# A graph layer with segment maxima: which engine makes the one-hot blocks of a slot's first and last chunk, when a search product is issued, and how a list's words are packed

## The chip, the cores and the metric

The kernel runs on one core of a Trainium2 chip. The metric is the device time of one execution in microseconds (us). TensorE is called PE in the profile, VectorE DVE, ScalarE ACT, GpSimd POOL and SyncE SP.

## The reference

```python
theta_x = (x[dst] - x[src]) @ theta_w.T + theta_b
phi_x = x[src] @ phi_w.T + phi_b
e = relu(theta_x + phi_x)
out = segment_max(e, dst, num_segments=6250)      # empty segments: 0
y = layernorm(x + out)
```

x has 6250 nodes of 256 features; there are 100,000 edges, sorted by dst. The part of an edge that depends on its source is a row of B = x @ (phi_w - theta_w).T, so what has to be done for each node is the maximum over its edges of gathered rows of B; the node's own product with theta_w and the biases are added after it.

## The kernel before, in words

The nodes come in two parts. The first 618 nodes (**part 1**) have their edges gathered row by row: POOL issues an indirect DMA for each step (`gather`, L527 to L538), and VectorE keeps a running maximum, one operation a step (`run_steps`, L690). The other 5632 nodes, 128 partitions x 44 (**part 2**), take two ways together:

- **Slots.** The source rows are cut into 17 slots of 383 rows. For each node at most one edge of each slot is chosen (`choice`, L1025, two slots at a time, all on VectorE). TensorE then fetches the chosen rows by products with one-hot matrices (`slot_halves`, L1095). A slot is worked in six chunks of nodes, five of 1024 and a last one of 512: 17 x 6 = 102 **parts** in a fixed order. For a chunk the chosen row numbers are loaded (`want`, L1108), a one-hot tensor `hot` of three blocks of 128 rows is made, and for each of two halves of the features 3 blocks x 2 terms x 2 widths = 12 matmuls go into a PSUM tile `ps_f` (6 for a chunk of 512); VectorE takes the maximum of it into `acc` (L1139; for the first slot ScalarE copies, L1137). The last slot has one block, not three. `hot` has two buffers, `ps_f` three.
- **The list.** Edges that no slot took are left over. VectorE packs them to a list: marks and a running count (L1232 to L1240), words with a distance (L1244 to L1257), eleven moves that close the gaps (L1261 to L1276), the owner's number (L1280). The words go to DRAM (L1283), POOL fetches each partition's 256 of them (L1291), and then issues 256 gathers of rows of B (`gather_2`, L1335), each followed by a short `pause` (an IOTA, L537). VectorE runs maxima over them (L699), two groups of eight behind the gathers. In the middle stage the program ties list and slots together: between two list steps it issues as many halves of chunks as the share of the list that is done asks for (`halves_until`), and VectorE's maxima and list steps are held in that order by hand.

When the list has ended its last rows are stored, POOL gathers the results of part 2 (44 gathers of `maxima`), and the shares of nodes are summed, normalised and stored. The last slot's six parts stand at the end of the slots, and VectorE takes their maxima after the list's last step.

**Who makes a hot block.** The number in `dve_hots[0]` says how many of the three blocks VectorE makes, with one comparison (L1114). ScalarE makes the rest in two operations: |row - number| for each block (L1116), then max(0, 1 - that) over all its blocks at once (L1119). The number is 0 for the first 19 parts (slots 0 to 2 and the first chunk of slot 3), 1 from there on, and is set to 0 again (L1582) when four groups of the list are left, which is ahead of the last seven parts before the last slot: slot 14's last chunk and all of slot 15. The trace has 70 such operations on VectorE.

**The search of places.** `node_place` (L855) finds where in part 1 the last edge of a node lies, in five calls: VectorE makes a hot (L858, L859), TensorE multiplies it with the edges' node numbers (L861), ScalarE counts by signs (L864) and copies (L867). A call stands at the end of each `next_group_1`, the step that also gathers and runs a group of part 1 and issues parts of slots.

Each engine takes its queue in order. What order that is, a scheduler decides when the program is built, from the order of the source, the dependencies and its own estimate of times; `behind_in_order` adds an edge to it without a wait.

Of the kernel before, what the change touches and what calls it, by code (L numbers as in the profile page):

```python
# [51 lines left out]
P = 128  # L52
# [383 lines left out]
def gnn_kernel(ctx: ExitStack, tc: tile.TileContext, x, src, dst, theta_w, theta_b, phi_w, phi_b, out):  # L436
# [418 lines left out]
    def node_place(j):  # L855
        cols = columns[:, j // Q1, :]
        hot = work.tile([P, P], FP, name="hot_1")
        nc.vector.tensor_scalar(hot, cols, low[:, j : j + 1], None, op0=ALU.is_ge)  # L858
        nc.vector.scalar_tensor_tensor(hot, cols, high[:, j : j + 1], hot, op0=ALU.is_lt, op1=ALU.mult)  # L859
        pp = misc()  # L860
        nc.tensor.matmul(pp[:, : T1 + 2], hot, ids_1[:, 1:], start=True, stop=True)  # L861
# [5 lines left out]
        nc.scalar.copy(origin[:, j : j + 1], pp[:, T1 + 1 : T1 + 2])  # L867

    def last_or_none(to, last_place, has, none):
        nc.vector.scalar_tensor_tensor(last_place, last_place, float(-none), has, op0=ALU.add, op1=ALU.mult)  # L870
# [68 lines left out]
    by_rank = "p (r j) -> p r j"  # L939
    by_node = "p (j r) -> p j r"  # L940
    words, work_1, work_2, order = (table(n) for n in ("words", "work_1", "work_2", "order"))
    node_part = index.tile([P, TILES, 1], FP, name="node_part")
    nc.gpsimd.iota(
        node_part, pattern=[[1 << 14, TILES], [0, 1]], base=0, channel_multiplier=0, allow_small_or_imprecise_dtypes=True
# [80 lines left out]
    def choice(s0):  # L1025
        n = min(BATCH_S, NS - s0)
        assert rows_in(s0) == rows_in(s0 + n - 1)
        W = TILES
        all_ranks = slice(0, CHOICE_R * W)
        in_slot = wide_i16(0, [P, BATCH_S, CHOICE_R * W])  # L1030
        for i in range(n):
            nc.vector.tensor_scalar(in_slot[:, i, :], padded[:, all_ranks], (s0 + i) * SLOT, None, op0=ALU.bitwise_xor)  # L1032
        lowest = wide_i16(BATCH_S * CHOICE_R * W, [P, BATCH_S, CHOICE_R * W // 2])

        low = lowest[:, :n, :]
        least = lambda to, a, b: nc.vector.tensor_tensor(to, a, b, op=ALU.min)  # L1036
# [9 lines left out]
        nc.vector.tensor_tensor(  # L1046
            kept[:, :n], kept[:, :n], at[:, :n].to_broadcast([P, n, CHOICE_R, W]), op=ALU.not_equal
        )
        for i in range(n):
            one = nc.vector.tensor_tensor(unused[:, all_ranks], unused[:, all_ranks], in_slot[:, i, :], op=ALU.mult)  # L1050
        ahead_of_run[0] = one.ins.name

# [42 lines left out]
    def slot_halves(s, c):  # L1095
# [12 lines left out]
        nc.sync.dma_start(want, flat(chosen_rows, s * OWN + begin, [[0, P], [1, wide_of]]))  # L1108
        hot = slots.tile([P, KB, CW], FR, name="hot")
        hot = hot[:, :, :wide_of]  # L1110
        of_dve = min(dve_hots[0], blocks)
        for b in range(blocks):
            if b < of_dve:
                nc.vector.tensor_scalar(hot[:, b, :], want, row_id[:, b : b + 1], None, op0=ALU.is_equal)  # L1114
# [114 lines left out]
        nc.vector.tensor_scalar(place_2, place_f, float(P * LIST), None, op0=ALU.min)  # L1229

    def list_pieces():
        left_over = wide_i16(3 * BATCH_S * CHOICE_R * TILES // 2, [P, TR])  # L1232
        nc.vector.scalar_tensor_tensor(left_over, padded, float(SLOT * NS), unused, op0=ALU.is_lt, op1=ALU.mult)
        valid, count = work_1, work_2
        nc.vector.tensor_copy(valid.rearrange(by_node, r=R), left_over.rearrange("p (r j) -> p j r", r=R))
        nc.vector.tensor_tensor_scan(count, valid, valid, 0.0, ALU.add, ALU.max)
        nc.vector.tensor_copy(n_list, count[:, TR - 1 :])
        sums = sums_of_lists()
        nc.vector.memset(up_to[:, 0:1], 0.0)
        nc.vector.tensor_copy(up_to[:, 1:], count.rearrange(by_node, r=R)[:, :, R - 1])  # L1240
# [3 lines left out]
        distance, mask = order.bitcast(I32), count.bitcast(I32)  # L1244
        nc.vector.tensor_tensor(distance, order, count, op=ALU.subtract)
        nc.vector.tensor_scalar(mask, valid, -1.0, None, op0=ALU.mult)
        word = words.bitcast(I32)
        nc.vector.tensor_tensor(
            word.rearrange(by_node, r=R),
            words.rearrange(by_node, r=R),  # L1250
            node_part.to_broadcast([P, TILES, R]),
            op=ALU.add,
        )
        done = valid.bitcast(I32)
        nc.vector.tensor_scalar(distance, distance, 20, None, op0=ALU.logical_shift_left)
        nc.vector.tensor_tensor(done, word, distance, op=ALU.bitwise_or)
        nc.vector.tensor_tensor(done, done, mask, op=ALU.bitwise_and)  # L1257
        yield

        moves = word  # L1260
# [206 lines left out]
    parts = [(s, c) for s in range(NS) for c in range(len(CHUNKS))]  # L1467
    groups_1 = list(range(X_GROUPS, len(groups)))
    todo = list(range(NT1))

    begun = [None]
    halves_of = len(parts) * 2
# [15 lines left out]
    def next_group_1(n):  # L1488
        if groups_1:
            i = groups_1.pop(0)  # L1490
            if held[0]:
                g_last, (t0, n_last) = ring_tiles[i - 1], groups[i - 1]
                for k in range(0, STEPS, 2):
                    run_steps(1, g_last, range(k, k + 2), caps_1, t0)
                    gather_group(i, b_rows, k, k + 2)
                    if k % 4 == 2 and n > k // 4:
                        fetch_parts(1)
                nc.sync.dma_start(maxima_1t[:, t0 : t0 + STEPS, :], g_last)
            else:
# [34 lines left out]
    while groups_1 or todo:  # L1534
        next_group_1(2)
    run_1(len(groups) - 1)
    places_1()
# [30 lines left out]
    for i in range(LIST_GROUPS):  # L1568
# [78 lines left out]
```

## Time and profile before

| what | value |
|---|---|
| median of 3 runs | 728.2 us (728.11 to 730.92) |
| the profiled execution's own time | 729.61 us |
| its span | 727.8 us |
| busy PE / DVE / ACT / POOL | 654.3 / 630.3 / 531.7 / 531.2 us |
| mean granted clock of TensorE | 0.966 |

In a row of a group of instructions stand: the line, the engine, the operation, what it writes and reads, the shapes and the number, then the busy time of all, the mean of one in ns, the idle time of the engine just before them, and what ended most of that. In a row of the timeline stand the start, the duration, the engine and the instruction, and in brackets the idle time before it with its releaser. In a row of stages stand the stretch and its length, the busy time of each engine (with its number of instructions), the granted clock, and the share and rate of the DMA engines. In a row of waits stand who waited for whom, the total in us, how often, and the longest.

### The profile page before, as it was taken

What the parts mean: (1) busy time and instruction counts of PE and PEld (TensorE: products, weight loads), DVE (VectorE), ACT (ScalarE), POOL (GpSimd) and SP (SyncE); (2) the same over time, 40 slices, a digit from 0 to 9 for tenths busy, and PEclk for the clock granted to TensorE, in tenths of its full rate; (3) what the DMA queues carried; (4) which work ended last, traced back from release to release, by engine and by line L of the source; (5) the groups of instructions that cost most, each with busy time, mean ns of one, the idle gap of its engine ahead of it and who ended that gap; (6) DMA issues with size and microseconds to landing.
All of it is one profiled execution on the core that took longest, in us unless ns stands there. A gap on an engine that the chain in (4) does not pass through costs nothing.

```text
span 727.8 us, 9889 instructions
## 1 busy us (share of the span) xinstructions
PE 654.3 (90%) x2908; PEld 530.6 (73%) x2908; DVE 630.3 (87%) x1193; ACT 531.7 (73%) x611; POOL 531.2 (73%) x730
## 2 busy tenths in 40 slices
PE   5799887769797999999999999999999988969990
PEld 3688765557576888888888888888888866748870
DVE  7999999989998788988889789898888984697876
ACT  1345788789896786877878778786876878852576
POOL 7700377888804888888888888888888888538880
PEclk9999999889999999999999999999999998999995
DMA  8898463736646676867777968886767675555875
GB/s 260 295 348 304 161 208 99 245 120 224 192 163 200 212 221 184 274 218 249 252 236 245 346 211 288 278 292 211 263 215 249 207 246 184 171 188 173 293 243 214
DMA packets 60879, 167.06 MB, mean 230 GB/s; under 512 B 11896, under 2 KB 21905, under 8 KB 54673
## 3 DMA queue, kind: packets, MB, share of 16 engines
q1 hardware_dynamic: 39717, 107.15, 42.6%
q0 software_dynamic: 18976, 52.35, 24.5%
q10 hardware_dynamic: 2124, 6.84, 2.5%
q8 instruction: 25, 0.41, 0.2%
q14 instruction: 37, 0.30, 0.1%
HBM read 102.94 MB, written 63.36 MB: 229 GB/s over the span
## 4 chain that ended last, share of the span: by engine, by line
PE 58%; DVE 17%; ACT 9%; POOL 6%; issue 5%; DMA 3%; DVEq 0%; SPq 0%; POOLq 0%; ACTq 0%
PE ps_f L1127 57%; POOL g L528 5%; ACT hot L1119 3%; ACT hot L1116 3%; DVE g L699 2%; DVE words L1003 2%; DVE wide L1036 2%; DVE work L1000 1%; POOL pause L498 1%; ACT x_f L1428 1%; DVE unused L1050 1%; DMA g<-maxima,place 1%; DVE wide L1046 1%; DMA dst_w<-in_dst_dram,window 1%; DVE wide L1032 1%
## 5 line engine op out<-in xcount | busy, mean ns | idle before, releaser
L1127 PE MATMUL ps_f<-hot,terms 128*128 128x512 f32 x2156 | 513.3, 398 | 28.4 <-ACT hot L1119 20.7
L1127 PEld LDWEIGHTS ps_f<-hot,terms 128*128 128x128 f32 x2156 | 407.8, 191 | 127.0 <-ACT hot L1119 30.5
L1116 ACT ACTIVATE hot<-want,minus_row 128x1024 fp32r<-128x1024 f16 (+1 forms) x224 | 228.9, 1071 | 94.7 <-PE ps_f L1127 94.6
L528 POOL DMA_INDIRECT g<-b_rows,list_src x256 | 257.9, 1008 | 50.3 <-issue 36.9
L1139 DVE TENSOR_TENSOR acc<-acc,ps_f 128x1024 f32<-128x1024 f32 x192 | 215.7, 1129 | 58.1 <-PE ps_f L1127 57.1
L1119 ACT ACTIVATE hot<-hot 128x2048 fp32r<-128x2048 f32 (+2 forms) x102 | 196.4, 1925 | 2.5
L699 DVE SCALAR_TENSOR_TENSOR g<-g,caps 128x256 f32<-128x256 f32 x335 | 161.2, 481 | 2.1
L528 POOL DMA_INDIRECT g<-b_rows,src x65 | 95.1, 1463 | 70.0 <-DMA b_rows<-b_sb 50.1
L498 POOL IOTA pause<- 128x160 f32 x312 | 97.6, 313 | 2.1
L794 PE MATMUL ps_b<-weights,x_t 128*128 128x256 f32 x260 | 60.9, 388 | 5.0 <-ACT x_t L782 4.4
L528 POOL DMA_INDIRECT g<-maxima,place x44 | 42.6, 969 | 25.1 <-DMA maxima<-g 18.2
L794 PEld LDWEIGHTS ps_b<-weights,x_t 128*128 128x128 f32 x260 | 48.5, 192 | 13.5 <-ACT x_t L782 7.5
L1114 DVE TENSOR_SCALAR hot<-want,row_id 128x1024 fp32r<-128x1024 f16 (+1 forms) x70 | 51.8, 739 | 0.3 <-issue 0.3
L1383 PE MATMUL ps_e<-weights,kept 128*128 128x256 f32 x176 | 41.5, 379 | 0.0
L1413 ACT ACTIVATE squares<-x_f,r 128x256 bf16<-128x256 f32 x49 | 24.2, 494 | 22.9 <-DVE r L1410 21.0
L797 ACT COPY b_sb<-ps_b 128x512 f32<-128x512 f32 (+1 forms) x25 | 14.4, 578 | 31.5 <-PE ps_b L794 20.1
L1383 PEld LDWEIGHTS ps_e<-weights,kept 128*128 128x128 f32 x176 | 33.4, 190 | 4.3
L1428 ACT ACTIVATE x_f<-x_f,r 128x256 f32<-128x256 f32 x41 | 21.3, 588 | 5.6 <-DVE r L1420 4.2
L782 ACT COPY x_t<-ps_xt 128x512 f32<-128x512 f32 (+1 forms) x33 | 18.3, 589 | 7.9 <-PE ps_xt L779 7.5
L528 POOL DMA_INDIRECT g<-in_x_dram,src x16 | 18.5, 1157 | 5.5 <-issue 4.1
L1393 DVE TENSOR_TENSOR g<-g,ps_e 128x512 f32<-128x512 f32 x22 | 15.1, 686 | 8.5 <-DMA g<-maxima,place 4.4
L521 POOL DMA_INDIRECT dst_w<-list_words,run_start x3 | 3.6, 1193 | 22.2 <-DMA list_words<-work 21.9
(255 smaller groups left out, 434.5 us busy)
## 6 DMA issues: line engine op xcount, KB each, us to landing
maxima<-g SPq DMA_DIRECT2D x42, 1024.0 KB
want<-chosen_rows SPq DMA_DIRECT2D x85, 256.0 KB
x_q<-in_x_dram SPq DMA_DIRECT2D x12, 512.0 KB
b_rows<-b_sb ACTq DMA_DIRECT2D x12, 512.0 KB
x_columns<-x_t SPq DMA_DIRECT2D x22, 256.0 KB
kept<-x_columns SPq DMA_DIRECT2D x11, 512.0 KB
raw<-b_rows SPq DMA_DIRECT2D x16, 256.0 KB
g<-b_rows,list_src POOLq DMA_INDIRECT x256, 4.1
```

The source lines that it names most:

```text
L498: return nc.gpsimd.iota(t, pattern=[[step, t.shape[1]]], base=base, channel_multiplier=per_partition, allow_small_or_imprecise_dtypes=True,)
L528: one = nc.gpsimd.indirect_dma_start(out=to, out_offset=None, in_=table, in_offset=bass.IndirectOffsetOnAxis(ap=offsets, axis=0))
L699: one = nc.vector.scalar_tensor_tensor(g[:, k, :], last[part], caps[:, t : t + 1], g[:, k, :], op0=ALU.min, op1=ALU.max)
L794: nc.tensor.matmul(ps[:, h, :], x_t[:, h, k, :], weights[:, k, 0, :], start=(k == 0), stop=(k == KC - 1))
L1114: nc.vector.tensor_scalar(hot[:, b, :], want, row_id[:, b : b + 1], None, op0=ALU.is_equal)
L1116: nc.scalar.activation(hot[:, b, :], want, AF.Abs, bias=minus_row[:, b : b + 1], scale=1.0)
L1119: nc.scalar.activation(apart, apart.bitcast(FP), AF.Relu, bias=1.0, scale=-1.0)
L1127: one = nc.tensor.matmul(ps[:, w : w + 512], terms[:, part, b, h * P : (h + 1) * P], hot[:, b, w : w + 512], start=(i == 0), stop=(i == n ...
L1139: one = nc.vector.tensor_tensor(to, to, ps, op=ALU.max)
L1383: nc.tensor.matmul(a[:, i, :], x_t[:, 2 * i + c, :], weights[:, c, 1, :], start=False, stop=(i == w - 1 and c == KC - 1))
L1413: nc.scalar.activation(squares, x_f[:, k, :], AF.Square, bias=mean[:, k : k + 1], scale=1.0, accum_out=var[:, k : k + 1])
L1428: nc.scalar.activation(x_f[:, k, :], x_f[:, k, :], AF.Identity, bias=mean[:, k : k + 1], scale=inv[:, k : k + 1])
```

## The change

Four edits, none of which changes a result:

1. **Hot blocks.** In a slot's first and last chunk VectorE makes one block always; the setting back to 0 near the list's end is gone, so the other chunks keep one block there too; and VectorE never makes the only block of a slot that has one. The 70 operations become 84: seven more in the first 19 parts (first or last chunks of slots 0 to 3), seven more near the list's end.
2. **Places.** `node_place` gives way twice. VectorE's hot is made at the end of a group's step, TensorE's product and ScalarE's counts at the end of the next group's step, and the product is ordered behind the slot product that was issued last.
3. **Choice.** For the first two slots the first comparison is written straight into `unused`, so that tensor is filled with ones only in its last third, and one multiplication goes; the comparison over two slots becomes two over one.
4. **The list's words.** Marks are made for the empty places rather than the taken ones, in one operation straight into the order by nodes; the running count of empty places is then the distance itself, and one operation masks it and one shifts it and joins it to the word.

```diff
@@ node_place
         nc.vector.scalar_tensor_tensor(hot, cols, high[:, j : j + 1], hot, op0=ALU.is_lt, op1=ALU.mult)
+        yield
         pp = misc()
-        nc.tensor.matmul(pp[:, : T1 + 2], hot, ids_1[:, 1:], start=True, stop=True)
+        one = nc.tensor.matmul(pp[:, : T1 + 2], hot, ids_1[:, 1:], start=True, stop=True)
+        if latest_product[0] is not None:
+            behind_in_order(one, latest_product[0], "slots ahead of the places")
...
@@ tables
-    nc.vector.memset(unused, 1)
+    nc.vector.memset(unused[:, CHOICE_R * TILES :], 1)
@@ choice
-        nc.vector.tensor_tensor(
-            kept[:, :n], kept[:, :n], at[:, :n].to_broadcast([P, n, CHOICE_R, W]), op=ALU.not_equal
-        )
-        for i in range(n):
+        first = unused[:, all_ranks].rearrange("p (s r j) -> p s r j", s=1, r=CHOICE_R)
+        for to, of in ((first, slice(0, 1)), (kept[:, 1:n], slice(1, n))) if s0 == 0 else ((kept[:, :n], slice(0, n)),):
+            nc.vector.tensor_tensor(
+                to, kept[:, of], at[:, of].to_broadcast([P, of.stop - of.start, CHOICE_R, W]), op=ALU.not_equal
+            )
+        for i in range(1 if s0 == 0 else 0, n):
             one = nc.vector.tensor_tensor(unused[:, all_ranks], unused[:, all_ranks], in_slot[:, i, :], op=ALU.mult)
@@ slot_halves
-        of_dve = min(dve_hots[0], blocks)
+        of_dve = min(1 if c in (0, len(CHUNKS) - 1) else dve_hots[0], blocks - 1)
@@ list_pieces
-        nc.vector.scalar_tensor_tensor(left_over, padded, float(SLOT * NS), unused, op0=ALU.is_lt, op1=ALU.mult)
-        nc.vector.tensor_copy(valid.rearrange(by_node, r=R), left_over.rearrange("p (r j) -> p j r", r=R))
-        nc.vector.tensor_tensor_scan(count, valid, valid, 0.0, ALU.add, ALU.max)
+        nc.vector.scalar_tensor_tensor(
+            empty.rearrange(by_node, r=R), of_nodes(padded), float(SLOT * NS), of_nodes(unused), op0=ALU.is_ge, op1=ALU.is_ge
+        )
+        nc.vector.tensor_tensor_scan(before_it, empty, empty, 0.0, ALU.add, ALU.max)
...
-        nc.vector.tensor_tensor(distance, order, count, op=ALU.subtract)
-        nc.vector.tensor_scalar(mask, valid, -1.0, None, op0=ALU.mult)
...
-        nc.vector.tensor_scalar(distance, distance, 20, None, op0=ALU.logical_shift_left)
-        nc.vector.tensor_tensor(done, word, distance, op=ALU.bitwise_or)
-        nc.vector.tensor_tensor(done, done, mask, op=ALU.bitwise_and)
+        nc.vector.scalar_tensor_tensor(distance, empty, 0.5, before_it, op0=ALU.is_lt, op1=ALU.mult)
+        nc.vector.scalar_tensor_tensor(
+            done, distance, 20, word, op0=ALU.logical_shift_left, op1=ALU.bitwise_or
+        )
...
-        nc.vector.tensor_scalar(done, done, (1 << 20) - 1, None, op0=ALU.bitwise_and)
-        one = nc.vector.tensor_tensor(done, done, owner.to_broadcast([P, OWN_LIST]), op=ALU.bitwise_or)
+        one = nc.vector.scalar_tensor_tensor(
+            done, done, (1 << 20) - 1, owner.to_broadcast([P, OWN_LIST]), op0=ALU.bitwise_and, op1=ALU.bitwise_or
+        )
@@ next_group_1
+        if searched[0] is not None:
+            next(searched[0])
+            searched[0] = None
         if todo:
-            node_place(todo.pop(0))
+            searched[0] = node_place(todo.pop(0))
+            next(searched[0])
@@ the list's loop
         if i == LIST_GROUPS - 4:
             list_places()
-            dve_hots[0] = 0
```

More of the change, by code (lines that the diff above doesn't have):

```diff
@@ L867, in node_place @@
         nc.scalar.copy(origin[:, j : j + 1], pp[:, T1 + 1 : T1 + 2])
+        yield
     def last_or_none(to, last_place, has, none):
@@ L941, in gnn_kernel @@
     words, work_1, work_2, order = (table(n) for n in ("words", "work_1", "work_2", "order"))
+    word = words.bitcast(I32)
     node_part = index.tile([P, TILES, 1], FP, name="node_part")
@@ L1231, in list_pieces @@
     def list_pieces():
[L1232 to L1235, printed above, removed]
-        nc.vector.tensor_tensor_scan(count, valid, valid, 0.0, ALU.add, ALU.max)
-        nc.vector.tensor_copy(n_list, count[:, TR - 1 :])
+        empty, before_it = work_1, work_2
+        of_nodes = lambda flags: flags.rearrange("p (r j) -> p j r", r=R)
+        nc.vector.scalar_tensor_tensor(
+            empty.rearrange(by_node, r=R), of_nodes(padded), float(SLOT * NS), of_nodes(unused), op0=ALU.is_ge, op1=ALU.is_ge
+        )
+        nc.vector.tensor_tensor_scan(before_it, empty, empty, 0.0, ALU.add, ALU.max)
+        nc.vector.tensor_scalar(n_list, before_it[:, TR - 1 :], -1.0, float(TR), op0=ALU.mult, op1=ALU.add)
         sums = sums_of_lists()
         nc.vector.memset(up_to[:, 0:1], 0.0)
-        nc.vector.tensor_copy(up_to[:, 1:], count.rearrange(by_node, r=R)[:, :, R - 1])
+        node_ends = lambda row: row.rearrange(by_node, r=R)[:, :, R - 1]
+        nc.vector.tensor_tensor(up_to[:, 1:], node_ends(order), node_ends(before_it), op=ALU.subtract)
         yield
@@ L1243, in list_pieces @@
         nc.vector.tensor_scalar(bad[:, 3:4], n_list, float(OWN_LIST), None, op0=ALU.is_gt)
[L1244 to L1247, printed above, removed]
+        by_nodes = lambda row: row.rearrange(by_node, r=R)
         nc.vector.tensor_tensor(
[L1249 to L1252, printed above, removed]
-        )
[L1254 to L1257, printed above, removed]
+            by_nodes(word), by_nodes(words), node_part.to_broadcast([P, TILES, R]), op=ALU.add
+        )
+        distance = order.bitcast(I32)
+        nc.vector.scalar_tensor_tensor(distance, empty, 0.5, before_it, op0=ALU.is_lt, op1=ALU.mult)
+        done = empty.bitcast(I32)
+        nc.vector.scalar_tensor_tensor(
+            done, distance, 20, word, op0=ALU.logical_shift_left, op1=ALU.bitwise_or
+        )
         yield
@@ L1469, in gnn_kernel @@
     todo = list(range(NT1))
+    searched = [None]
     begun = [None]
@@ L1533, in gnn_kernel @@
     kept_ring = body.enter_context(tc.tile_pool(name="kept_ring", bufs=3, side="right"))
-    while groups_1 or todo:
+    while groups_1 or todo or searched[0] is not None:
         next_group_1(2)
```

## The prediction

> **What bounds the kernel now.** I read the chain that ended last first, then the busy times by stage.
>
> ```profile
> PE 58%; DVE 17%; ACT 9%; POOL 6%; issue 5%; DMA 3%; DVEq 0%; SPq 0%; POOLq 0%; ACTq 0%
> ```
> ```profile
> 120.00:150.00 30.00, 19.40 (x70) 15.21 (x70) 29.41 (x67) 23.38 (x37) 24.78 (x17) 0.82 0.59 204
> 150.00:180.00 30.00, 26.62 (x106) 21.04 (x107) 27.69 (x37) 27.83 (x30) 25.42 (x16) 0.89 0.46 150
> 180.00:210.00 30.00, 25.88 (x109) 19.49 (x108) 30.00 (x44) 27.32 (x20) 16.33 (x11) 1.00 0.60 191
> ...
> 228.00:550.00 322.00, 321.90 (x1410) 263.00 (x1411) 278.64 (x470) 250.61 (x220) 279.99 (x420) 0.99 0.76 245
> 550.00:597.00 47.00, 47.00 (x208) 38.53 (x207) 39.96 (x59) 35.56 (x30) 41.14 (x63) 1.00 0.71 224
> ```
>
> The columns are the stretch, its length, then busy time of PE, PEld, DVE, ACT and POOL. Over the whole run PE leads, but the stages have different limits. From 120 to 210 us VectorE (DVE) is busy 29.4, 27.7 and 30.0 of each 30 us: the list of left-over edges is made there. From 228 to 597 us PE is busy without a gap, and 208 matmuls take 47.0 us, 0.226 us each. The next rows show what starts and ends the middle stage.
>
> ```profile
> 231.91 0.95 POOL L528 DMA_INDIRECT g<-b_rows,list_src  x1 [5.83 <-DVE dst_w L1301]
> ```
> ```profile
> 627.83 0.95 POOL L528 DMA_INDIRECT g<-b_rows,list_src  x1 [0.16 <-issue]
> ...
> 647.23 0.95 POOL L528 DMA_INDIRECT g<-maxima,place  x1 [18.16 <-DMA maxima<-g]
> ```
> ```profile
> 642.27 0.42 DVE L697 TENSOR_TENSOR g<-g,heads 128x256 f32<-128x256 f32 x1
> ```
> ```profile
> 559.76 38.03 PE L1127 MATMUL ps_f<-hot,terms 128*128 128x512 f32 x166
> ...
> 602.08 13.48 PE L1127 MATMUL ps_f<-hot,terms 128*128 128x512 f32 x48 [4.17 <-ACT hot L1119]
> ...
> 628.13 10.34 PE L1127 MATMUL ps_f<-hot,terms 128*128 128x512 f32 x44 [0.23 <-ACT hot L1119]
> ```
>
> The list's gathers run on GpSimd (POOL) from 231.9 to 627.8 us. The list's last step on VectorE ends at 642.27 + 0.42 = 642.7 us, its rows are stored, and POOL, idle for 18.16 us, begins the last gathers only then. So the end follows two times: when the list's gathers can start (set by VectorE), and when the list ends. Just before the end PE stands still 4.17 us for a hot of ScalarE (ACT), and the next 48 matmuls take 13.48 us instead of 48 x 0.226 = 10.8.
>
> **The change part by part. The tail.** The last seven chunks before the last slot now keep a DVE block.
>
> ```profile
> L1116 ACT ACTIVATE hot<-want,minus_row 128x1024 fp32r<-128x1024 f16 x186 | 203.6, 1143 | 79.2 <-PE ps_f L1127 79.0
> L1119 ACT ACTIVATE hot<-hot 128x2048 fp32r<-128x2048 f32 x59 | 113.1, 1917 | 1.4
> L1119 ACT ACTIVATE hot<-hot 128x3072 fp32r<-128x3072 f32 x21 | 58.2, 2770 | 0.4
> L1114 DVE TENSOR_SCALAR hot<-want,row_id 128x1024 fp32r<-128x1024 f16 x59 | 46.3, 785 | 0.3 <-issue 0.3
> L1114 DVE TENSOR_SCALAR hot<-want,row_id 128x512 fp32r<-128x512 f16 x11 | 5.5, 496 | 0.0
> ```
>
> A wide chunk without DVE costs ACT 3 x 1.143 + 2.770 = 6.2 us against 24 x 0.226 = 5.4 us of PE; with DVE it is 2 x 1.143 + 1.917 = 4.2 us, and ACT is hidden behind PE. Slot 15 has 5 x 24 + 12 = 132 matmuls. PE is free for them at 559.76 + 38.03 = 597.8 us, and they end at about 628.13 + 36/44 x 10.34 = 636.6. Without a gap they take 132 x 0.226 = 29.8 us and end at 627.6: PE alone would give 9.0 us. DVE takes 6 x 0.785 + 0.496 = 5.2 us more; the stage from 550 to 597 us, with a DVE block in most chunks, shows DVE at 39.96 of 47 us, so there is room.
>
> What is late next is POOL, whose gathers feed the same steps.
>
> ```profile
> g<-b_rows,list_src POOLq DMA_INDIRECT x256, 4.1
> ```
> ```profile
> 550.00:597.00 47.00, 30.96 (x32) 1.00 0.71 224
> 597.00:629.00 32.00, 21.84 (x23) 0.89 0.64 206
> ```
> ```profile
> 550.00:597.00 47.00, 10.18 (x31) 1.00 0.71 224
> 597.00:629.00 32.00, 6.44 (x23) 0.89 0.64 206
> ```
> ```profile
> 302.75 0.82 DVE L1114 TENSOR_SCALAR hot<-want,row_id 128x1024 fp32r<-128x1024 f16 x1
> ```
> ```profile
> 303.06 0.67 POOL L498 IOTA pause<- 128x160 f32 x1
> ```
>
> The two pairs are POOL's gathers (L528) and pauses (L498) in two stages. A gather and its pause take 0.968 + 0.328 = 1.296 us where DVE makes hots, and 0.950 + 0.280 = 1.230 us where it makes none; the pause at 303 us, under a hot, took 0.67. Over 32 gathers and some 8 hots the difference is 0.066 x 32 / 8 = 0.27 us per hot (the seven more cost POOL 1.9 us). The last gather then goes out at 627.8 + 1.9 and lands 4.1 later; a step and the end, put at the 0.42 of the row at 642.27 each, give 634.6 at the earliest. PE's bound is 642.7 - 9.0 = 633.7. The later one counts: **tail -8.1 us**.
>
> The Trainium skill, "SBUF — State Buffer", section "Who interferes with whom", says of this pair of engines that VectorE in a two-port mode and GpSimd block each other for whole instructions. It speaks against the change; that GpSimd is stretched agrees, that it is by the whole instruction does not (0.27 us against 0.785). By the rule the tail would give about 4.8 us in place of 8.1; it is the first rival below.
>
> **The early part.** DVE bounds it, so its own work counts.
>
> ```profile
> L1050 DVE TENSOR_TENSOR unused<-unused,wide 128x1056 int16<-128x1056 int16 x17 | 12.0, 706 | 0.5
> L1046 DVE TENSOR_TENSOR wide<-wide,at 128x2112 int16<-128x2112 int16 x8 | 10.0, 1252 | 0.0
> L1046 DVE TENSOR_TENSOR wide<-wide,at 128x1056 int16<-128x1056 int16 x1 | 0.7, 701 | 0.0
> ```
> ```profile
> L1233 DVE SCALAR_TENSOR_TENSOR wide<-padded,unused 128x1584 int16<-128x1584 int16 x1 | 1.8, 1802 | 0.0
> L1235 DVE CAST work<-wide 128x1584 f32<-128x1584 int16 x1 | 1.9, 1916 | 0.0
> L1245 DVE TENSOR_TENSOR order<-order,work 128x1584 int32<-128x1584 f32 x1 | 1.8, 1792 | 0.0
> L1246 DVE TENSOR_SCALAR work<-work 128x1584 int32<-128x1584 f32 x1 | 1.1, 1068 | 0.0
> L1255 DVE TENSOR_SCALAR order<-order 128x1584 int32<-128x1584 int32 x1 | 1.0, 969 | 0.0
> L1256 DVE TENSOR_TENSOR work<-words,order 128x1584 int32<-128x1584 int32 x1 | 1.8, 1795 | 0.0
> L1257 DVE TENSOR_TENSOR work<-work,work 128x1584 int32<-128x1584 int32 x1 | 1.8, 1792 | 0.0
> L1007 DVE SCALAR_TENSOR_TENSOR padded<-work,words 128x1584 int16<-128x1584 f32 x1 | 3.0, 3036 | 0.0
> ```
>
> - Choice: one multiplication (0.706) goes, and the comparison of two slots becomes two of one, 2 x 0.701 - 1.252 = +0.15. -0.55 us. The shorter fill lies at the start, where DVE waits for inputs anyway: nothing.
> - List front: 1.802 + 1.916 go, one operation over two re-ordered inputs comes. It is not in the trace: 1.80 (L1233, same count, contiguous) to 3.04 (L1007, two re-ordered inputs). I take 3.04, since its inputs are re-ordered too: -0.68, at best -1.9.
> - List words: 1.792 + 1.068 + 0.969 + 1.795 + 1.792 = 7.42 go, two of SCALAR_TENSOR_TENSOR come. Between 1.80 and 3.04 each; I take 1.80, as they are contiguous: -3.8, at worst -1.3. Merging the last two small ones is set at nothing.
> - DVE blocks before the list is ready: of the first 19 parts, seven are first or last chunks, 4 wide and 3 narrow: 4 x 0.785 + 3 x 0.496 = **+4.6**.
>
> Sum of DVE's work: -0.4 us. Then its waits:
>
> ```profile
> PE ps L861 <- DVE hot L859: 5.1, 1, 5.1
> ...
> DVE acc L1139 <- PE ps_f L1127: 2.3, 2, 1.2
> ```
> ```profile
> POOL dst_w L521 <- DMA list_words<-work: 21.9, 1, 21.9
> ```
>
> PE stood 5.1 us on a search product (L861) whose hot came late from DVE. The product now goes behind a slot's products, one group later, with its three ACT operations; it issues no DMA, and no transfer is moved past SP's or POOL's queue. That lets PE's results, and with them DVE's maxima, come earlier: between 0 and 2.3 us of DVE's waits; I take 1.6. POOL waits 21.9 us for the list's words, so what DVE gains there passes on to the gathers in full. **Early part -2.0 us**, bounds from +1.8 (dear operations, no wait removed) to -4.7 (cheap front, all waits).
>
> **Sum.** -8.1 - 2.0 = -10.1 us on the profiled execution's 729.6 us (its span is 727.8; 1.8 us lie around it): 719.5. That execution lies 1.4 us above the median of the runs shown, 728.2, so the predicted time is 718.1.
>
> **The rivals.** (1) *POOL is held for whole hots.* Each hot would cost POOL its own length, 5.2 us in the tail instead of 1.9: the tail gives 4.8, the sum is -6.8, **721.4**. For it: the pauses stretched under hots; against it: the mean of 0.27. (2) *The early DVE blocks stall the engine that bounds the stage.* A hot has two buffers, so hot n must wait until PE has done with part n-2. VectorE takes its queue in order; behind a waiting hot stand the list's moves, the steps of the first part and the maxima, and POOL and PE wait for these. Half a part's products are 12 x 0.226 = 2.7 us; seven such waits are 19 us, against 10.1 gained: **737**. It decides from 1.4 us a wait. For it: seven hots come into a queue that was full. Against it: while DVE is the late one, PE has mostly done with old parts, and the hots made in the middle stage sat idle 0.3 us in all. (3) *The tail doesn't get faster*: the hots on DVE come behind its ordered steps and maxima, and PE waits for them instead of for ACT. Only the early part is left: **726**. Against it: the middle stage runs that way without a gap on PE.
>
> **How the numbers follow.** A measurement of this kernel tells about 0.5%, 3.6 us, from no change. Forecast 0.62 (its own range 714 to 721), rival 1 0.16, rival 3 0.11, rival 2 0.11. The first two are faster: 0.78; rival 3 is the same: 0.11; rival 2 slower: 0.11. The range goes from PE's bound and the best early part (728.2 - 9.0 - 4.7 = 714.5) to rival 1 with the worst early part (728.2 - 4.8 + 1.8 = 725.2); it leaves out rival 2 and most of rival 3.
>
> **What would show it.** Tail: no PE wait for a hot after 597 us, last list gather to last list step some 7 us instead of 15. POOL: a gather and its pause near 1.30 us to the end. Early: the first list gather 2 us before 231.9; DVE's new operations at 3.0, 1.8 and 1.8 us; no search product with a wait of 5 us. It is wrong if the first list gather comes later than 231.9 (rival 2 or dear operations) or if the list ends later than 637 + that shift.

## The result: 0.6% faster, less than half of the forecast

The changed kernel takes 725.1 us (median of 17 runs, 721.6 to 727.6), the kernel before, beside it, 728.75 us. The ratio is 0.9938, 95% interval 0.9925 to 0.9951: 4.5 us faster where 10.1 were forecast. The profiled execution of the changed kernel has a span of 721.3 us (before 727.8) and took 723.1 us.

The profile after, in the order of the prediction. The timeline of POOL, changed kernel: the first and the last gather of the list, and the first gather of the last stage.

```profile
226.13 0.96 POOL L528 DMA_INDIRECT g<-b_rows,list_src  x1 [7.79 <-DVE dst_w L1307]
...
628.28 0.95 POOL L528 DMA_INDIRECT g<-b_rows,list_src  x1 [0.16 <-issue]
...
640.42 0.95 POOL L528 DMA_INDIRECT g<-maxima,place  x1 [10.90 <-DMA maxima<-g]
```

The timeline of DVE, changed kernel: the list's last step.

```profile
635.45 0.42 DVE L697 TENSOR_TENSOR g<-g,heads 128x256 f32<-128x256 f32 x1
```

The list starts 5.8 us earlier than in the kernel before (226.13 against 231.91) and ends 6.8 us earlier (635.87 against 642.69). Yet its last gather comes no earlier (628.28 against 627.83): what was gained at the start is gone before the end.

The timeline of PE, changed kernel, at the list's end (lines 1134 and 1126 are what 1127 and 1119 were):

```profile
558.66 72.91 PE L1134 MATMUL ps_f<-hot,terms 128*128 128x512 f32 x319
...
632.09 1.19 PE L1134 MATMUL ps_f<-hot,terms 128*128 128x512 f32 x4 [0.40 <-ACT hot L1126]
```

PE no longer stands still for ScalarE's hots; it runs without a gap to 631.5 us. That PE, not POOL, is now last is shown below by its products and by POOL's waits. The stages of the early part, changed kernel:

```profile
120.00:150.00 30.00, 21.06 (x75) 16.43 (x74) 29.98 (x70) 21.45 (x29) 24.78 (x16) 0.82 0.53 187
150.00:180.00 30.00, 26.76 (x111) 21.07 (x110) 29.67 (x38) 28.53 (x30) 25.61 (x15) 0.95 0.58 181
180.00:210.00 30.00, 24.81 (x98) 19.13 (x98) 29.66 (x47) 22.76 (x23) 14.59 (x11) 0.94 0.54 180
```

DVE (third busy time) is no less full than before, though its list work became shorter. The groups of its new operations, changed kernel:

```profile
L1241 DVE SCALAR_TENSOR_TENSOR work<-padded,unused 128x1584 f32<-128x1584 int16 x1 | 3.7, 3669 | 0.0
L1260 DVE SCALAR_TENSOR_TENSOR work<-order,words 128x1584 int32<-128x1584 int32 x1 | 1.8, 1799 | 0.0
L1258 DVE SCALAR_TENSOR_TENSOR order<-work,work 128x1584 int32<-128x1584 f32 x1 | 1.8, 1794 | 0.0
```

The waits from 90 to 250 us, changed kernel (total, how often, the longest):

```profile
POOL dst_w L521 <- DMA list_words<-work: 16.1, 1, 16.1
...
PE ps_f L1134 <- DVE hot L1121: 9.4, 4, 4.0
```

The second row is new: in the early part PE waits 9.4 us for hots that DVE makes late. The timeline of PE, changed kernel, shows the two longest of these, both at the last chunk of a slot (12 products), and one more wait. L912 are the transposes of part 1's last running maximum (`tails_1`); they wait for the last step of part 1 on DVE:

```profile
148.76 4.58 PE L1134 MATMUL ps_f<-hot,terms 128*128 128x512 f32 x12 [3.49 <-DVE hot L1121]
...
189.77 4.58 PE L1134 MATMUL ps_f<-hot,terms 128*128 128x512 f32 x12 [4.00 <-DVE hot L1121]
...
221.26 0.69 PE L912 MATMUL ps<-ident,g 128*128 128x128 f32 x2 [2.58 <-DVE g L699]
```

The experiments below ran on five occasions, on which the kernel before itself took 755.7, 765.3, 729.7, 753.3 and 729.2 us; so each ratio is against the kernel before on the same occasion, and traces are compared between the occasions of 729 us and the first profiles, or on one occasion.

### The profile page after: what moved, and what is told of

It reads as the page before. It is cut to its first block, busy times and chain, and to the rows that moved or that the text cites. A ratio compares the mean times of both kernels' runs of the same rounds, so it can differ in the third digit from the quotient of the medians.

```text
span 721.3 us, 9888 instructions
## 1 busy us (share of the span) xinstructions
PE 653.8 (91%) x2908; PEld 532.9 (74%) x2908; DVE 634.1 (88%) x1202; ACT 510.1 (71%) x597; POOL 526.9 (73%) x730
## 4 chain that ended last, share of the span: by engine, by line
PE 62%; DVE 17%; POOL 6%; DMA 5%; ACT 5%; issue 4%; ACTq 0%; DVEq 0%; POOLq 0%
PE ps_f L1134 60%; POOL g L528 4%; DVE g L699 3%; DVE words L1008 2%; ACT hot L1123 1%; ACT hot L1126 1%; DVE work L1005 1%; POOL pause L498 1%; ACT x_f L1434 1%; DVE wide L1041 1%; DMA g<-maxima,place 1%; DMA dst_w<-in_dst_dram,window 1%; DMA dst<-in_dst_dram 1%; DMA dst_w<-list_words,run_start 1%; DMA list_words<-work 1%
## 5 line engine op out<-in xcount | busy, mean ns | idle before, releaser
L1123 ACT ACTIVATE hot<-want,minus_row 128x1024 fp32r<-128x1024 f16 x210 | 216.4, 1078 | 100.9 <-PE ps_f L1134 100.9
L1126 ACT ACTIVATE hot<-hot 128x2048 fp32r<-128x2048 f32 (+2 forms) x102 | 186.6, 1829 | 2.6
L528 POOL DMA_INDIRECT g<-b_rows,src x65 | 92.1, 1418 | 69.6 <-DMA b_rows<-b_sb 49.8
L1121 DVE TENSOR_SCALAR hot<-want,row_id 128x1024 fp32r<-128x1024 f16 x84 | 61.6, 734 | 0.3 <-issue 0.3
L1419 ACT ACTIVATE squares<-x_f,r 128x256 bf16<-128x256 f32 x49 | 24.2, 494 | 21.9 <-DVE r L1416 21.9
L1144 ACT COPY acc<-ps_f 128x1024 f32<-128x1024 f32 (+1 forms) x12 | 11.3, 941 | 14.6 <-PE ps_f L1134 14.6
```

The source lines that it names most:

```text
L528: one = nc.gpsimd.indirect_dma_start(out=to, out_offset=None, in_=table, in_offset=bass.IndirectOffsetOnAxis(ap=offsets, axis=0))
L1123: nc.scalar.activation(hot[:, b, :], want, AF.Abs, bias=minus_row[:, b : b + 1], scale=1.0)
L1126: nc.scalar.activation(apart, apart.bitcast(FP), AF.Relu, bias=1.0, scale=-1.0)
L1419: nc.scalar.activation(squares, x_f[:, k, :], AF.Square, bias=mean[:, k : k + 1], scale=1.0, accum_out=var[:, k : k + 1])
```

## The experiments

The change has four separable edits. The tail (T) and the early hots (H) are in two lines, each shown against the kernel before:

```diff
 T: seven chunks at the list's end keep a DVE block
             list_places()
-            dve_hots[0] = 0
-        of_dve = min(dve_hots[0], blocks)
+        of_dve = min(dve_hots[0], blocks - 1)
```
```diff
 H: hots of VectorE in a slot's first and last chunk
-        of_dve = min(dve_hots[0], blocks)
+        of_dve = min(1 if c in (0, len(CHUNKS) - 1) else dve_hots[0], blocks - 1)
```

N is the search of places in steps (the two yields in `node_place`, the order behind `latest_product`, and `searched`). W is the choice and the list's words in fewer operations. The whole change is T+H+N+W.

| run | edits | kernel before there | ratio | 95% interval |
|---|---|---|---|---|
| e1 | T | 755.7 | 0.9894 | 0.9861 to 0.9927 |
| e2 | H, not at the tail | 755.7 | 1.0051 | 1.0020 to 1.0083 |
| e3 | T+N+W | 755.7 | 0.9988 | 0.9953 to 1.0022 |
| e4 | T+H+W | 755.7 | 0.9850 | 0.9798 to 0.9902 |
| e5 | T+H+N+W | 765.3 | 0.9871 | 0.9805 to 0.9937 |
| e6 | T+W | 765.3 | 1.0052 | 1.0002 to 1.0103 |
| e7 | W | 765.3 | 1.0150 | 1.0090 to 1.0210 |
| e8 | N | 765.3 | 0.9994 | 0.9961 to 1.0026 |
| g1 | none | 729.7 | 1.0003 | 0.9984 to 1.0022 |
| g2 | T | 729.7 | 0.9903 | 0.9874 to 0.9932 |
| g3 | T+H | 729.7 | 1.0011 | 0.9991 to 1.0032 |
| g4 | T+H+N+W | 729.7 | 0.9938 | 0.9913 to 0.9963 |
| h1 | T+N+W | 753.3 | 0.9912 | 0.9857 to 0.9966 |
| h2 | T+W | 753.3 | 0.9994 | 0.9956 to 1.0032 |
| h3 | T + list words of W | 753.3 | 0.9908 | 0.9866 to 0.9950 |
| h4 | T+N+W, hots in first chunks | 753.3 | 0.9822 | 0.9783 to 0.9860 |
| j1 | as h4 | 729.2 | 0.9873 | 0.9849 to 0.9896 |
| j2 | T+N+W | 729.2 | 0.9953 | 0.9938 to 0.9969 |

**The parts, one at a time (e1 to e4).** Expected of the tail alone:

> The kernel before with one edit: the number of DVE blocks is not set back to 0 near the list's end (slot 14's last chunk and slot 15 keep one). Theory A (PE is the bound from the list's start to its end, so PE time saved in the tail comes through in full; what the whole change lacks was lost by PE in the early part): 7 to 9 us faster than before, PE without a wait for a hot after 597 us, list end near 634. Theory B (the list's gathers on POOL set the end, and the seven added hots slow them): 3 to 4 us faster, the last list gather as late as before or later, and VectorE's list steps waiting for rows.

Of the early hots alone (the line of H, with `and not pinned[0]`, so that the list's stage stays as it was):

> The kernel before with one edit: VectorE makes a block in the first and last chunk of the first 19 parts (seven blocks); the tail is as before. Theory A: these hots come late in a full VectorE queue, PE waits for them some 4 us at the narrow chunks, 2 to 4 us slower than before. Theory B: what counts is when the list starts; seven hots are 4.6 us of VectorE, ACT is freed, within 1 us of before or up to 4 us slower with the first list gather 4 us later.

Of the change without the early hots (the line of H taken back to that of T):

> The changed kernel without the blocks in first and last chunks of the first 19 parts; tail, places, choice and list words as changed. Theory A: 2 to 4 us faster than the changed kernel (ratio to before 0.988 or lower), no PE wait for a DVE hot before 220 us. Theory B: within 1 us of the changed kernel, or faster only by what the list starts earlier.

Of the change without the steps of the search:

> The changed kernel with the search of places as before (hot, product and counts together). Theory A: the 5 us wait of PE for the search's hot returns, 0 to 2 us slower than the changed kernel. Theory C (the later products and ScalarE's counts among a slot's operations cost more than the wait did): 1 to 3 us faster than the changed kernel.

The tail was confirmed: e1 gained 1.06%, about 8 us. The early hots alone cost 0.5%. But the change without them was not faster: e3 keeps hardly anything of the tail's gain. The change without the steps of the search gained 1.5% (e4). So prices of single edits do not add up: the hots cost alone, and taking them out of the whole does not bring that price back. That they help beside W is not shown here, since the whole change was not run on this occasion.

**The parts of the early edits (e5 to e8).**

> The changed kernel as it is, beside the others of this call, so that they can be compared on one chip. If the tail alone is worth 1.1% and early hots alone cost 0.5%, and the rest adds nothing: 0.6% faster than before, as measured first. It is the reference for the other three.

> The changed kernel without early hots and with the search of places as before: tail, choice and list words only. Theory C (the later place products are what costs; the words start the list earlier): 1.2 to 1.8% faster than before, better than the changed kernel by 0.5% or more. Theory A' (PE bounds from the list's start on, so a list that starts earlier gives nothing): as the tail alone, 1.0 to 1.1% faster.

> The kernel before with choice and list words as changed, nothing else. If VectorE's work in the early part counts in full: 5 us of work less, 0.5 to 0.7% faster, first list gather 4 to 6 us earlier. If PE bounds: within 0.3% of before, although the list starts earlier.

> The kernel before with only the search of places split, its product behind the slot products one group later. Theory C: 0.4 to 0.9% slower than before. As I predicted (PE's 5 us wait goes): 0.1 to 0.4% faster, no PE wait for the search's hot.

The whole change stands at 0.9871 here (e5), where 0.9938 was measured first and again later (g4); the change without early hots stands at 0.9988, 0.9912 and 0.9953 on three occasions (e3, h1, j2). So the ratio of one kernel moves by up to 0.8% between occasions, and what follows rests on kernels of one occasion, or of the two on which the kernel before took 729 to 730 us. The search of places in steps does nothing by itself (e8). The shorter choice and words alone made the kernel slower by 1.5% (e7); beside the tail e6 lies 1.6% above e1, but on another occasion. Fewer VectorE operations, slower kernel: that is the open point that the next runs were chosen for.

**The tail, the early hots and the whole side by side (g1 to g4).**

> The kernel before, unchanged, for its profile on this occasion. Both theories: ratio 1.000 within 0.3%. Its products of TensorE done by 230 us are the base for the others (418 in the first profile of the kernel before, 408 in that of the changed kernel).

> Only the seven chunks at the list's end keep a DVE block; everything before them is as in the kernel before. Theory E (TensorE's products decide, and the early part of the change costs TensorE about 2 us): 8 to 9 us faster, ratio about 0.988, and 2 to 3 us faster than the whole change on the same chip. Theory F (the start of the list's gathers decides, as the prediction had it): also about 8 us faster, but 2 us or more slower than the whole change.

> The tail and the hots of VectorE in a slot's first and last chunk, without the other search of places and without the shorter list words. Theory E: the early hots come late and TensorE waits for them; 0.3 to 0.8% slower than the tail alone, as the early hots alone were 0.5% slower than the kernel before. Theory F: the list starts about 4 us later than in the kernel before and the whole gives only about 4 us (ratio 0.994). A third reading (the early hots help by taking work from ScalarE, whose order the rest of the change had spoilt): equal to the tail alone or better.

> The whole change once more, beside the tail alone on the same chip. Theory E: 0.994 here, 2 to 3 us slower than the tail alone, with fewer products done by 230 us than the kernel before. Theory F: 0.986, faster than the tail alone by what the list starts earlier.

The tail alone takes 722.7 us and the whole change 725.3: everything but the tail costs about 2.6 us (the two intervals just overlap). The early hots beside the tail alone cost 7.9 us (g3, 730.6), 1.1% where theory E gave 0.3 to 0.8%. Four views of each kernel say why. First the tail alone: the products of TensorE in two stretches of the early part and to 600 us (the stages for the tile ps_f: stretch, length, busy time, number of products, granted clock, DMA share and rate).

```profile
90.00:210.00 120.00, 90.06 (x347) 0.93 0.55 177
210.00:250.00 40.00, 35.35 (x148) 0.96 0.67 215
250.00:600.00 350.00, 345.70 (x1505) 1.00 0.77 245
```

Its first and last list gather on POOL's timeline:

```profile
230.51 0.95 POOL L528 DMA_INDIRECT g<-b_rows,list_src  x1 [5.90 <-DVE dst_w L1301]
...
628.62 1.13 POOL L528 DMA_INDIRECT g<-b_rows,list_src  x1 [0.16 <-issue]
```

And its last list steps on DVE's:

```profile
634.03 1.01 DVE L699 SCALAR_TENSOR_TENSOR g<-g,caps 128x256 f32<-128x256 f32 x2 [3.02 <-DMA g<-b_rows,list_src]
635.07 0.42 DVE L697 TENSOR_TENSOR g<-g,heads 128x256 f32<-128x256 f32 x1
```

Now the tail with the early hots (g3), the same views, with its waits of PE from 90 to 235 us:

```profile
90.00:210.00 120.00, 81.87 (x285) 0.83 0.54 175
210.00:250.00 40.00, 36.96 (x158) 1.00 0.67 209
```
```profile
PE ps_f L1127 <- DVE hot L1114: 16.4, 4, 5.2
```
```profile
230.52 0.96 POOL L528 DMA_INDIRECT g<-b_rows,list_src  x1 [6.53 <-DVE dst_w L1301]
```
```profile
643.85 0.42 DVE L697 TENSOR_TENSOR g<-g,heads 128x256 f32<-128x256 f32 x1
```

The two lists start at the same moment, 230.5 us. The early hots cost the list's start nothing, although the prediction charged them 4.6 us of it. They cost PE: 443 products by 250 us instead of 495. PE waits 16.4 us for hots that stand late in DVE's queue. Its other waits are shorter, so the time in these products is only 6.6 us less (118.8 against 125.4); at the tail's 0.253 us a product 118.8 us would hold some 469, an estimate, and the other half of the 52 is lost to the rate, at a granted clock of 0.83 against 0.93 up to 210 us. And the list ends 8.8 us later. This is what tells the two theories apart: the end follows the products that PE has behind it (theory E), not the start of the list (theory F).

The whole change again (g4):

```profile
90.00:210.00 120.00, 86.95 (x328) 0.90 0.55 178
210.00:250.00 40.00, 34.43 (x140) 0.91 0.64 205
```
```profile
226.31 0.96 POOL L528 DMA_INDIRECT g<-b_rows,list_src  x1 [8.30 <-DVE dst_w L1307]
```
```profile
638.34 0.42 DVE L697 TENSOR_TENSOR g<-g,heads 128x256 f32<-128x256 f32 x1
```

Its list starts 4.2 us before that of the tail alone, but PE has 468 products by 250 us, 27 fewer, and the list ends 3.3 us later. Executions of the same early code differ too: 489 and 488 products in the two profiles of the kernel before, 495 in the tail alone, which has the same early part, and 480 in the first profile of the whole change. So a difference of a dozen products says nothing about the code. The 52 of the early hots lie far beyond that; the whole change has 27 fewer than the tail alone here and 15 in its first profile.

**What of the words and what of the hots (h1 to h4, j1 and j2).**

> The whole change without its hots of VectorE in first and last chunks (tail, places and words stay); on an occasion on which the kernel before takes about 729 us. Theory E (the early hots on VectorE come late and TensorE waits for them): faster than the whole change, since the tail alone is at 0.990 and the earlier list takes off up to 2.9 us more, that is 0.986 to 0.990. Theory G (in the order that the shorter words bring about, ScalarE makes its hots late, and the early hots only repaired that): 0.995 to 1.000, with waits of TensorE for ScalarE's hots between 110 and 130 us.

> The tail and the words and choice in fewer operations, the search of places as in the kernel before. Theory E: as h1 or a little slower, 0.986 to 0.992. Theory G: 0.995 to 1.005.

> The tail and the list words alone: the choice of slots keeps its operations, so ScalarE's order in the choice stage stays near that of the kernel before. Theory E: 0.986 to 0.990. Theory G, if the choice's shorter operations are what changes ScalarE's order: 0.986 to 0.990 here and h2 slower than it by over 1%; if the list words do it, this is as slow as h2.

```diff
 h4: hots of VectorE in first chunks only
-        of_dve = min(1 if c in (0, len(CHUNKS) - 1) else dve_hots[0], blocks - 1)
+        of_dve = min(1 if c == 0 else dve_hots[0], blocks - 1)
```

> The whole change, but VectorE makes an early hot only in a slot's first chunk, not in its last (three early hots fewer). Theory E: the waits for hots of last chunks (two of about 4 us each in the profile of the changed kernel) go, 1 to 4 us faster than the whole change. Theory G: no faster than the whole change, between it and h1.

> The whole change with early hots in first chunks only, on another occasion. If the hots of last chunks are what cost (theory E): faster than the tail alone was, 0.980 to 0.988 here (714 to 720 us where the kernel before takes 729), with the list's first gather near 221 us and about 500 products of TensorE done by 250 us. Otherwise 0.992 or slower, as the whole change.

> The whole change without early hots, on the same occasion as j1. Theory E: as fast as j1 or faster. Theory G (the shorter choice changes ScalarE's order, and TensorE waits for ScalarE's hots; hots of VectorE in first chunks repair it): 0.6% or more slower than j1, with waits of TensorE for ScalarE's hots between 110 and 130 us.

With the choice's operations as they were (h3) the tail and the list words gain 0.9%; with the choice shortened too (h2) nothing is left. The 1 to 4 us that theory E gave the version with hots in first chunks did come, and more: 0.9822 and 0.9873, **720.1 us**, 9.2 us faster than the kernel before. Its interval lies wholly below that of the whole change (0.9913 to 0.9963, g4), and overlaps with that of the tail alone (g2). The kernel without early hots stayed at 0.9953, as fast as the whole change. The views of j1:

```profile
90.00:210.00 120.00, 86.69 (x328) 0.89 0.60 188
210.00:250.00 40.00, 39.60 (x171) 1.00 0.66 208
```
```profile
217.15 0.96 POOL L528 DMA_INDIRECT g<-b_rows,list_src  x1 [6.93 <-DVE dst_w L1307]
...
623.85 0.95 POOL L528 DMA_INDIRECT g<-b_rows,list_src  x1 [0.16 <-issue]
```
```profile
631.03 0.43 DVE L697 TENSOR_TENSOR g<-g,heads 128x256 f32<-128x256 f32 x1
```

With its waits of PE from 90 to 235 us and two rows of PE's timeline:

```profile
PE ps_f L1134 <- DVE hot L1121: 11.7, 2, 5.9
```
```profile
151.89 13.09 PE L1134 MATMUL ps_f<-hot,terms 128*128 128x512 f32 x48 [5.86 <-DVE hot L1121]
...
192.48 13.29 PE L1134 MATMUL ps_f<-hot,terms 128*128 128x512 f32 x48 [5.83 <-DVE hot L1121]
```

Theory E's figures for j1 came in full (0.980 to 0.988, about 500 products), but not by its mechanism. The waits for VectorE's hots did not go: they moved from the last chunks to the first chunks behind them and total 11.7 us, where g4 has 9.5. By 210 us j1 has the 328 products that g4 has. The gain lies behind 210 us, 171 products against 140 (h4, the same kernel on its occasion, has 12.1 us of such waits and 171 products too). There g4 has a wait that j1 has not; the first row is of g4's DVE, the second of its PE:

```profile
222.13 0.49 DVE L1301 COPY_PREDICATED dst_w<-words,dst_w 128x290 int32<-128x290 int32 x1 [5.52 <-DMA dst_w<-list_words,run_start]
```
```profile
223.04 0.69 PE L912 MATMUL ps<-ident,g 128*128 128x128 f32 x2 [5.03 <-DVE g L699]
```

DVE stands 5.52 us for the list's words that POOL fetches; behind that operation in its queue stands the last step of part 1, for which PE waits. In j1 the last operation on the words (L1285) starts at 202.88 instead of 207.72 us, POOL's first fetch of them at 206.12 instead of 213.74, and neither DVE nor PE waits there.

And of j2, with two rows of PE's timeline:

```profile
90.00:210.00 120.00, 88.50 (x346) 0.91 0.57 184
210.00:250.00 40.00, 32.43 (x129) 0.91 0.67 210
```
```profile
219.67 1.33 POOL L528 DMA_INDIRECT g<-b_rows,list_src  x1 [5.41 <-DVE dst_w L1307]
```
```profile
636.73 0.42 DVE L697 TENSOR_TENSOR g<-g,heads 128x256 f32<-128x256 f32 x1
```
```profile
216.57 0.44 PE L912 MATMUL ps<-ident,g 128*128 128x128 f32 x2 [3.08 <-DVE g L699]
...
231.10 23.45 PE L1134 MATMUL ps_f<-hot,terms 128*128 128x512 f32 x96 [4.30 <-ACT hot L1126]
```

j2 has the list 10.8 us earlier than the tail alone and as many products by 210 us (346 against 347). It has 19 fewer between 210 and 250: PE waits 3.08 us for the last step of part 1 (L912), and then 4.30 us for a wide first chunk, slot 3's, whose hot ScalarE makes whole. In j1 VectorE makes a block of that chunk, the list comes 2.5 us earlier still, and from 217.97 to 627 us PE has no wait at all; its 171 products in this stretch are the most of all. Theory E had the kernel without early hots at 0.986 to 0.990 (h1) and as fast as j1, and fell with j2's 0.9953; theory G foresaw that loss, but by waits at 110 to 130 us, and by 210 us j2 has lost no products. What is left of both is one rule.

**One number gives the end.** From 250 to 600 us each changed kernel makes 1505 or 1506 products in 345.7 us, 0.2295 us each; nothing differs there. So the products missing at 250 us set the end of the list, unless POOL is later. Reckoned from j1 (499 products, end 631.46):

| kernel | first list gather | products 90 to 250 us | missing x 0.2295 | end reckoned | end measured |
|---|---|---|---|---|---|
| T (g2) | 230.51 | 495 | 0.9 | 632.4 | 635.49 |
| whole, first profile | 226.13 | 480 | 4.4 | 635.8 | 635.87 |
| T+N+W (j2) | 219.67 | 475 | 5.5 | 637.0 | 637.15 |
| whole (g4) | 226.31 | 468 | 7.1 | 638.6 | 638.76 |
| T+H (g3) | 230.52 | 443 | 12.9 | 644.3 | 644.27 |

Four of five agree within 0.2 us, in no order of the list's start. (A product across 210 us counts in both stretches; that is one or two in each kernel, and without it they still agree.) The exception is the tail alone: there POOL is last. Its row at 634.03 shows DVE's last list steps waiting 3.02 us for rows, and 635.49 less 3.02 is 632.5. POOL's own waits from 235 to 640 us tell the same, first in the tail alone, then in j2:

```profile
POOL g L528 <- DVE g L699: 5.0, 20, 1.9
```
```profile
POOL g L528 <- DVE g L699: 18.3, 27, 14.1
```

In the other four it waits 10.5 to 18.3 us (in j1 15.8) for DVE's steps before it can gather on: POOL runs ahead and then stands. j1 is first because its products are the most and its list is early enough for POOL (623.85 + 6.9 = 630.7).

## Why the prediction was wrong, and where it was right

- **Tail: right, 1.0 us too large.** Forecast -8.1 us, measured -7.05, in the times (729.72 to 722.67) and in the list's end (g1's last step ends at 642.54, g2's at 635.49). POOL is the later engine there, as forecast, and its 256 gathers take 1.59 us longer (398.11 in g2 against 396.52 in g1; 395.92 in the first profile of the same kernel), 0.23 us for each of the seven hots where 0.27 was forecast. With it the first rival falls, which needed 5.2 us. (Its 5.2 counts six wide hots and one narrow; the trace has five and two, 4.9 us.) The Trainium skill, "SBUF — State Buffer", section "Who interferes with whom", says that VectorE in a two-port mode and GpSimd block each other for the whole instruction; by that a wide hot could hold POOL for up to 0.785 us, which the trace doesn't bear out, and whether these hots run in such a mode no view here shows. What was too small is the way from the last gather's issue to the list's end: 4.9 us in the working (4.1 of landing and two steps of 0.42), 6.9 measured.
- **Early part: the step that failed.** "POOL waits 21.9 us for the list's words, so what DVE gains there passes on to the gathers in full. **Early part -2.0 us**". It did pass on to the gathers, and more was gained than forecast (-5.8 us at the first gather). But the sum then took the gathers' gain for the end's, while with the tail made faster PE sets the end: POOL waits 10.5 us in the changed kernel, and PE has 480 and 468 products by 250 us where the kernel before has 489 and 488. Measured in the times, the early part is +2.6 us (g4 against g2). The tail's own working could have told: with PE's bound at 633.7 and POOL's at 634.6, an earlier list alone can give 0.9 us at most. The bounds of this part, +1.8 and -4.7, also don't come out of its terms, which give +2.1 and -3.9.
- **The early hots were priced as DVE's busy time, 4.6 us of the list's start.** Beside the tail alone they move that start by nothing and cost 7.9 us, through the products that PE is late with; the middle stage has no gap in which PE could make them up. The length of PE's waits for them is not the price either: 16.4 us in g3, 9.4 in the change, 11.7 in j1, the fastest. Rival 2 named the place (in-order VectorE in the stage that was full) but with another wait (a hot waiting for its buffer) and a price of 19 us.
- **Operations.** The list front took 3.67 us, above both bounds (1.80 to 3.04); the two of the words 1.79 and 1.80, as taken. The search product's wait of 5 us went, as forecast; e8 shows no gain from the steps of the search alone.
- **Signs in the profile.** No wait of PE for a hot between 597 and 631 us, and 7.6 us from the last gather to the list's end: right. A gather and its pause near 1.30 us to the end: right, 1.31 from 597 us on. The first list gather 2 us earlier: right in sign; it was read as a sign of the end, and it is one only where POOL is last. The sign of failure came: the list had to end by 637 plus the shift of the first gather, 631.2, and ended at 635.9.
- **Rival 3** falls with g2: the seven late hots are not late for PE. That its 726 lies near the measured 725.1 is chance: it kept the early gain and lost the tail's, and the runs show the reverse.

Open: the three hots of last chunks and j1's lack of them are 9 us apart in the list's start (226.13 against 217.15), far more than their 0.5 to 0.7 us each; 4.8 to 5.5 us of it are there when the words are done (L1285, at 202.88 against 207.72 in g4 and 208.38 in the first profile); the order of DVE's and POOL's queues differs between the two kernels, and no run isolates which place of it does this. Nor was it isolated why the shortened choice costs 0.9% (h2 against h3), or why choice and words alone cost 1.5% (e7): there the first list gather goes out at 247.26 us, in e8, on the same occasion, at 239.33, so with less work for VectorE the list came later. And the change without the steps of the search (e4, 0.9850) was not run beside the whole one; on one occasion these steps are worth 0.8% beside the tail and W (h1 against h2, whose intervals overlap a little), so whether they help or cost in the whole is open.

## What to carry to other kernels

When a change speeds up one of two engines that share an end, work out the end by both, each with all parts of the change: here the gathers' start was right and it was the wrong clock. An operation moved to a full, in-order engine costs not its duration but the work that the engine using its result is then late with, so count the consumer's work done at the point from which it runs without a gap; from j1's count that one number gave the end of four other executions to 0.2 us, and it missed the one in which another engine was last. The same rule cost in one place and paid in another: blocks on VectorE in last chunks went with the slower kernel, and with the block in slot 3's first chunk PE's wait of 4.30 us is gone, so try such a rule place by place.

## What the runs showed of the hardware

A wait of PE can cost more than its length. In g4 PE waits 5.03 us from 218 us on; the stages after it, for all instructions, then in j1, which has no wait there:

```profile
223.04:227.00 3.96, 3.96 (x11) 3.19 (x12) 3.75 (x12) 0.00 (x0) 0.69 (x1) 0.50 0.18 63
227.00:231.00 4.00, 4.00 (x16) 3.25 (x15) 2.29 (x8) 0.00 (x0) 3.50 (x7) 0.83 0.40 116
```
```profile
218.34:222.30 3.96, 3.96 (x18) 3.29 (x18) 3.96 (x17) 3.27 (x4) 3.48 (x6) 1.00 0.81 260
```

The granted clock is 0.50 for 4 us after the wait, and 11 instructions take the time of 18; the next 132 products take 32.76 us in g4 and 30.48 in j1, so by this comparison the wait of 5.0 us cost 7.3. The Trainium skill, "TensorE: Matmul & The Clock Gate", section "What's actually happening", says that the clock falls to half after an idle window of about 3.4 us and returns after a busy one; these rows agree. A shorter wait did it too: in the first profile of the changed kernel the stage after the wait of 2.58 us at 221 us has a clock of 0.60, so its rows don't bear the 3.4 us out.

```profile
221.26:225.20 3.94, 3.94 (x12) 3.23 (x13) 2.44 (x7) 0.00 (x0) 0.00 (x0) 0.60 0.29 112
```

The prediction read such a row at the tail (48 matmuls in 13.48 us instead of 10.8), but its rivals took waits at their length. The second unexpected number is the list front's: an operation that reads two 16-bit inputs in another order than they are stored in and writes 32-bit in order (L1241) took 3.67 us for 1584 elements a row; the one over contiguous 16-bit inputs in the kernel before (L1233) took 1.80.
